# Small loads as rows on one partition, edges first in the queue, and a first tile in halves, in a GNN and FFN layer on one core

## The chip, the core and the metric

The kernel runs on one core of a Trainium2 chip. A core has TensorE (matrix products, PE in the profile, its weight loads PEld), VectorE (DVE), ScalarE (ACT), GpSimd (POOL) and SyncE (SP), each with an instruction stream of its own, worked in order; they wait for one another through semaphores. Loads and stores are issued by SP and GpSimd here and moved by 16 DMA engines. SBUF has 128 partitions; products go to PSUM. The metric is the device time of one execution in microseconds (us); less is better.

## The reference, cut to what matters

`x` is 384 x 1024 in f32. A graph attention layer and a quantised FFN are each added to it, after a layer norm without weights.

```python
x = x + gnn(_layernorm(x), [src, dst], edge_type_5, edge_type_weights, wq, bq, ... wo, bo)
x = x + ffn(_layernorm(x)[None], clip_x, clip_down, w_gate, w_up, w_down)[0]

# gnn: 16 heads of 64
q = x @ wq.T + bq                     # k and v alike
q2 = (q @ wiq.T + biq)                # k2 and v2 alike, by heads
w = softplus(edge_type_weights)       # 4 values
mask = full(-inf); mask[src, dst] = w[edge_type - 1]     # 6528 edges, the last of equal ones stays
scores = q2 @ k2.T * 0.125 + mask
out = softmax(scores) @ v2 @ wo.T + bo
# ffn: activations and weights rounded to 8 bits
scale = sigmoid(clip) * max(abs(x)) / 127                # clip: one value for x, one for the inner product
```

`edge_type_weights` has four values and the two clips one each. They are needed on all 128 partitions, as operands for each partition of later instructions.

## The kernel before

The 384 rows of `x` are three tiles of 128 rows (`NT`), the 1024 columns eight chunks of 128 (`KC`).

**The opening** (lines 83 to 358). SP issues the loads of x and of the first blocks of wq (lines 84 to 87, `load_w` at 77): x tiles 0 and 1, two blocks of wq, x tile 2, then more of wq, 512 KB each. GpSimd issues small ones (lines 100 to 105): the 40 rows of biases, the four edge weights spread to all partitions by a source that repeats (`row_bcast`, line 57), the two clips likewise, and three loads of edge indices, 51 rows of 128 values each. For each tile, `row_stats` (line 277) takes mean and variance on VectorE, a square root on ScalarE and a refinement on VectorE; `normalise` (line 284) writes the normalised row in two halves on VectorE, TensorE transposes it chunk by chunk into two PSUM tiles of four chunks, and ScalarE copies each into `xnT` (line 296). Between the two groups of a tile `normalise` calls `between`, which puts other work into the engines' streams: for tile 0 the statistics of tile 1, and for tile 1 `edges_and_stats` (line 317): the conversion of the edges, their keys, the store and loads that spread the keys, and the statistics of tile 2. `q_first` (line 300) then multiplies the tile by a block of wq: two blocks for each tile, eight products each. Each f32 product makes two records on TensorE.

Before this TensorE transposes the identity 36 times (line 311). After the third tile come the edge weights' small steps (lines 333 to 340), the transpose of the biases (line 342), the sums for the next wq pair (`left_sums`), the copy of the biases (line 346), the sums of x (`right_sums`, tile `x_right`), and the last products of the first pair (lines 349 to 358).

**Behind it** (lines 443 to 480) 15 pairs of blocks follow, seven products of half size for each (`project2`, line 189), with one step of "aside" work after each: tables for the edge weights, then the search for equal edges on VectorE (line 412) and the scatter of each 128 edges by GpSimd (line 425). The attention stage (line 541) computes scores, softmax and weighting for pairs of heads, with the last projections and the FFN's weights filled in; then come the output projection, the second norm and the FFN.

The order on TensorE, SP and GpSimd is that of the program throughout (line 74). On VectorE and ScalarE it is so from the opening to the end of line 480's loop (line 266) and again at the tail (line 726); between, a planner orders these two engines.

Of the kernel before, what the change touches and what calls it, by code (L numbers as in the profile page):

```python
# [23 lines left out]
F32 = mybir.dt.float32  # L24
# [8 lines left out]
P = 128  # L33
N = 384
NT = N // P
F = 1024
KC = F // P
# [19 lines left out]
def row_bcast(ap, n):  # L57
    return bass.AP(tensor=ap.tensor, offset=ap.offset, ap=[[0, P], [1, n]])
# [3 lines left out]
def gnn_ffn_kernel(ctx: ExitStack, tc: tile.TileContext, a: dict, out: bass.AP):  # L62
    nc = tc.nc

    const = ctx.enter_context(tc.tile_pool(name="const", bufs=1))
# [6 lines left out]
    ps_tp = ctx.enter_context(tc.tile_pool(name="ps_tp", bufs=2, space=PSUM))  # L72
# [4 lines left out]
    def load_w(name, j):  # L77
        wt = w.tile([P, F], F32, name="wt")
        nc.sync.dma_start(wt, a[name][j])
        return wt  # L80


    x = act.tile([P, NT, F], F32, name="actT")
    for t in range(NT):
        if t == NT - 1:
            wq_first = [load_w("wq", o) for o in range(FIRST)]
        nc.sync.dma_start(x[:, t, :], a["x"][t * P : (t + 1) * P, :])
    bias_rows = const.tile([5 * KC, P], F32)
    etw = const.tile([P, 4], F32)
    clip = const.tile([P, 2], F32)  # L90
    biv_b = const.tile([P, F], F32)


    ident = const.tile([P, P], F32)
# [2 lines left out]
    ph1_stack = ExitStack()  # L97
    ph1 = ph1_stack.enter_context(tc.tile_pool(name="ph1", bufs=2))
    edges_i = ph1.tile([EC, 3, P], I32, name="edges_i", bufs=1)
    nc.gpsimd.dma_start(bias_rows, a["biases"])  # L100
    nc.gpsimd.dma_start(etw, row_bcast(a["L0_gnn_edge_type_weights"], 4))
    nc.gpsimd.dma_start(clip[:, 0:1], row_bcast(a["L0_ffn_clip_x"], 1))
    nc.gpsimd.dma_start(clip[:, 1:2], row_bcast(a["L0_ffn_clip_down"], 1))
    for j, name in enumerate(("src", "dst", "edge_type_5")):
        nc.gpsimd.dma_start(edges_i[:, j, :], a[name].rearrange("(c p) -> c p", p=P))

    ahead = ph1.tile([P, GROUP * P], F32, name="ahead", bufs=1)
    nc.gpsimd.iota(ahead, pattern=[[1, GROUP * P]], base=0, channel_multiplier=-1, allow_small_or_imprecise_dtypes=True)
# [31 lines left out]

    ident_b = const.tile([P, P], BF16)
    later = ph1.tile([P, GROUP * P], F32, name="later", bufs=1)
    bias = const.tile([P, 5 * KC], F32)
    w8 = const.tile([P, 4], F32)

    def right_sums(src, pool, name, in_place=True):
# [15 lines left out]
    def left_sums(wa, wb, pool):  # L162

        half = HK * P
        s1 = pool.tile([P, half], F32, name="s1")
        s2 = pool.tile([P, half], F32, name="s2")

        def steps():
            nc.vector.tensor_add(s1, wb[:, :half], wb[:, half:])
            yield  # L170
            nc.vector.tensor_sub(s2, s1, wa[:, :half])
            yield
            nc.vector.tensor_sub(wb[:, :half], wa[:, :half], wb[:, :half])
            yield

        return (s1, s2), steps()
# [60 lines left out]
    def run(steps):  # L237
        for _ in steps:
            pass


    xnT = act.tile([P, KC, N], F32, name="actT")
# [3 lines left out]
    with ph1_stack:  # L246
# [37 lines left out]
        def normalise(t, between=None):  # L284
            xn = rows_p.tile([P, F], F32, name="row")
            for j in range(2):
                hs = slice(j * 512, (j + 1) * 512)
                nc.vector.tensor_scalar(
                    xn[:, hs], x[:, t, hs], mv1[:, t, 0:1], rstd1[:, t : t + 1], op0=ALU.subtract, op1=ALU.mult
                )  # L290
            for g in range(2):
                pt = ps_tp.tile([P, 4, P], F32, name="tp")
                for j in range(4):
                    c = 4 * g + j
                    nc.tensor.transpose(pt[:, j, :], xn[:, c * P : (c + 1) * P], ident)
                nc.scalar.copy(xnT[:, 4 * g : 4 * g + 4, t * P : (t + 1) * P], pt)
                if g == 0 and between:
                    between()

# [9 lines left out]
        pt = ps_tp.tile([P, P], F32, name="tp")  # L309
# [19 lines left out]
        q_first(0, 1)  # L329
        q_first(1, 1)  # L330
        normalise(2)

        wneg = small.tile([P, 4], F32, name="wneg")
        nc.vector.tensor_scalar(wneg, etw, -1.0, None, op0=ALU.mult)
# [3 lines left out]
        nc.scalar.activation(wexp, wnab, AF.Exp)  # L338
        wln = small.tile([P, 4], F32, name="wln")
        nc.scalar.activation(wln, wexp, AF.Ln, bias=1.0)  # L340
        pt = ps_tp.tile([P, 512], F32, name="tp")
        nc.tensor.transpose(pt[:, : 5 * KC], bias_rows, ident[: 5 * KC, : 5 * KC])
        wq_next = [load_w("wq", o) for o in (2, 3)]
        sums_next, steps = left_sums(*wq_next, ph1)
        run(steps)
        nc.vector.tensor_copy(bias, pt[:, : 5 * KC])
        x_right, steps = right_sums(xnT, ph1, "x_right", in_place=False)
        run(steps)
        q_first(0, 2)
# [2 lines left out]
        pt = ps_tp.tile([P, 3, EC], F32, name="tp")  # L352
# [102 lines left out]
        for i, (name, o) in enumerate(todo[:-1]):  # L455
# [9 lines left out]
            wq_next = [load_w(todo[i + 1][0], todo[i + 1][1] + j) for j in range(2)]  # L465
            sums_next, steps = left_sums(*wq_next, turned if todo[i + 1][0] == "wik" else ph1)
# [3 lines left out]
            if name == "wv" and o >= KC - 4:  # L470
                steps = in_turn(steps, islice(q_steps, 4))
# [69 lines left out]
    with ExitStack() as ph:  # L541
# [122 lines left out]
        for p in range(NP):  # L664
# [4 lines left out]
            if p == NP - 1:  # L669
                early = [(t, g, ps_mm.tile([P, 512], F32, name="mm")) for t, g in ((0, 0), (0, 1))]  # L670
                fill, n = (s for t, g, pm in early for s in out_group(wo, t, g, range(NP - 2), pm)), 2 * (NP - 2)
            elif p % 2:
                k2_next, fill = inner_k(p + 1)
                n = 7 * HK + 1
            else:
                fill, n = inner_v(p // 2), NT * KC
# [305 lines left out]
```

## Time and profile before

Three executions took 386.22, 386.88 and 388.01 us, median 386.88. One more, taken with the profiler, took 387.15 us; its span from the first instruction to the last is 385.4 us, so 1.75 us lie around it. The granted TensorE clock was 0.997.

| engine | busy us | share of the span | instructions |
|---|---|---|---|
| PE | 363.4 | 94% | 2100 |
| PEld | 299.4 | 78% | 2101 |
| DVE | 262.2 | 68% | 785 |
| ACT | 107.0 | 28% | 256 |
| POOL | 79.5 | 21% | 81 |

TensorE leads; in the chain that ended last it has 81% of the span, VectorE 11%, ScalarE 4%, DMA 1%. Over the first 25 us, the stage that the change edits, TensorE is busy 0.65 of the stage from 1 to 2 us (with the transposes of the identity), 0.30 of the one from 7 to 8, and full or nearly so from 11 on. A busy share over the whole span says little about this stage; it has to be read from its own lines. In a line of the timeline the columns are start, length, engine, line, operation, what it writes and reads, and, in brackets, how long the engine had been idle and what released it.

### The profile page before, as it was taken

What the parts mean: (1) busy time and instruction counts of PE and PEld (TensorE: products, weight loads), DVE (VectorE), ACT (ScalarE), POOL (GpSimd) and SP (SyncE); (2) the same over time, 40 slices, a digit from 0 to 9 for tenths busy, and PEclk for the clock granted to TensorE, in tenths of its full rate; (3) what the DMA queues carried; (4) which work ended last, traced back from release to release, by engine and by line L of the source; (5) the groups of instructions that cost most, each with busy time, mean ns of one, the idle gap of its engine ahead of it and who ended that gap; (6) DMA issues with size and microseconds to landing.
All of it is one profiled execution on the core that took longest, in us unless ns stands there. A gap on an engine that the chain in (4) does not pass through costs nothing.

```text
span 385.4 us, 5844 instructions
## 1 busy us (share of the span) xinstructions
PE 363.4 (94%) x2100; PEld 299.4 (78%) x2101; DVE 262.2 (68%) x785; ACT 107.0 (28%) x256; POOL 79.5 (21%) x81
## 2 busy tenths in 40 slices
PE   7999999999999999899899999999989999998972
PEld 7899999999999999798686767768766445457660
DVE  5878888888789977995747376546662421298775
ACT  2252100000000100325545553555243423001430
POOL 6100354454445553830000000000000000000003
PEclk9999999999999999999999999999999999999998
DMA  7996333343433355274030504050573000000004
GB/s 236 376 378 229 112 111 109 113 129 111 116 120 124 134 168 201 78 230 134 30 129 1 167 0 128 8 177 2 199 292 85 26 0 2 0 0 1 2 1 163
DMA packets 17804, 44.50 MB, mean 115 GB/s; under 512 B 3262, under 2 KB 8400, under 8 KB 17392
## 3 DMA queue, kind: packets, MB, share of 16 engines
q1 hardware_dynamic: 15104, 39.46, 30.2%
q0 software_dynamic: 2672, 4.68, 4.0%
q8 instruction: 16, 0.26, 0.3%
q14 instruction: 12, 0.10, 0.1%
HBM read 41.91 MB, written 2.21 MB: 115 GB/s over the span
## 4 chain that ended last, share of the span: by engine, by line
PE 81%; DVE 11%; ACT 4%; DMA 1%; issue 1%; POOL 0%; POOLq 0%; ACTq 0%; DVEq 0%
PE p L189 35%; PE mm L577 11%; PE mm L189 8%; PE sc L600 4%; PE sc L638 3%; PE sc L648 3%; PE mm L648 3%; PE tp L630 3%; PE mm L303 3%; DVE e L620 2%; ACT e L610 2%; ACT eTs L632 1%; PE mm L791 1%; PE x L838 1%; DVE s L606 1%
## 5 line engine op out<-in xcount | busy, mean ns | idle before, releaser
L425 POOL DMA_INDIRECT mask_d<-value,place x51 | 64.2, 1259 | 65.3 <-DVE place L422 49.9
L189 PE MATMUL p<-actT,wt 128*128 128x192 f32 x360 | 66.0, 326 | 0.5 <-DVE wt L210 0.5
L189 PEld LDWEIGHTS p<-actT,wt 128*128 128x128 f32 x360 | 59.6, 190 | 0.8 <-DVE wt L210 0.8
L577 PE MATMUL mm<-wt,actT 128*128 128x256 f32 x192 | 45.9, 386 | 0.0
L610 ACT ACTIVATE e<-s,mn 128x384 f32<-128x384 f32 x48 | 29.1, 606 | 54.3 <-DVE mn L606 54.3
L577 PEld LDWEIGHTS mm<-wt,actT 128*128 128x128 f32 x192 | 35.0, 190 | 7.9 <-issue 2.2
L606 DVE CUSTOM_DVE_ANT_0 s<-sc,mask 128x384 f32<-128x384 f32 x48 | 24.4, 552 | 14.5 <-PE sc L600 13.8
L808 POOL MEMSET hT<- 128x384 f32 x1 | 0.4, 417 | 158.6 <-PE sc L638 158.6
L189 PE MATMUL p<-x_right,s 128*128 128x192 f32 x176 | 32.2, 326 | 0.0
L189 PE MATMUL p<-x_right,wt 128*128 128x192 f32 x176 | 32.2, 326 | 0.0
L189 PEld LDWEIGHTS p<-x_right,s 128*128 128x128 f32 x176 | 29.2, 190 | 0.0
L189 PEld LDWEIGHTS p<-x_right,wt 128*128 128x128 f32 x176 | 29.2, 190 | 0.0
L632 ACT COPY eTs<-tp 128x384 f32<-128x384 f32 x48 | 20.6, 480 | 26.3 <-PE tp L630 26.2
L412 DVE SCALAR_TENSOR_TENSOR junk<-key_b,key,later 128x384 f32<-128x384 f32 (+3 forms) x51 | 27.5, 540 | 0.0
L200 DVE SCALAR_TENSOR_TENSOR actT<-p,bias,actT 128x192 f32<-128x192 f32 x45 | 18.7, 416 | 8.4 <-PE p L189 5.1
L203 ACT COPY actT<-p 128x192 f32<-128x192 f32 x15 | 4.8, 318 | 66.1 <-PE p L189 66.1
L600 PE MATMUL sc<-k,actT 64*128 64x384 f32 x96 | 22.7, 522 | 0.2 <-DVE actT L642 0.2
L630 PEld LDWEIGHTS tp<-ident,e 128*128 128x128 f32 x144 | 17.2, 140 | 4.3 <-issue 2.6
L213 ACT ACTIVATE actT<-p,bias 128x192 f32<-128x192 f32 x15 | 6.3, 421 | 50.8 <-issue 28.7
L189 PE MATMUL mm<-actT,wt 128*128 128x192 f32 x96 | 20.1, 337 | 0.3 <-ACT k L203 0.3
L501 DVE CAST wqi<-w8b 128x352 bf16<-128x352 int8 (+2 forms) x14 | 6.9, 491 | 18.8 <-PE tp L537 9.8
L630 PE MATMUL tp<-ident,e 128*128 128x128 f32 x144 | 19.6, 273 | 0.0
(210 smaller groups left out, 593.9 us busy)
## 6 DMA issues: line engine op xcount, KB each, us to landing
wt<-in_wq_dram SPq DMA_DIRECT2D x8, 512.0 KB
wt<-in_wk_dram SPq DMA_DIRECT2D x8, 512.0 KB
wt<-in_wv_dram SPq DMA_DIRECT2D x8, 512.0 KB
wt<-in_wiq_dram SPq DMA_DIRECT2D x8, 512.0 KB
wt<-in_wik_dram SPq DMA_DIRECT2D x8, 512.0 KB
wt<-in_wiv_dram SPq DMA_DIRECT2D x8, 512.0 KB
wt<-in_wo_dram SPq DMA_DIRECT2D x8, 512.0 KB
actT<-in_x_dram SPq DMA_DIRECT2D x6, 512.0 KB
```

Source lines behind the costliest of these rows:

```text
L189: nc.tensor.matmul(z, left[:, k * P : (k + 1) * P], r[:, k, :], start=(k == 0), stop=(k == HK - 1))
L200: nc.vector.scalar_tensor_tensor(dst, z, b, with_, op0=ALU.add, op1=ALU.add)
L303: nc.tensor.matmul(pm_first[o][:, ts], wq_first[o][:, k * P : (k + 1) * P], xnT[:, k, ts], start=(k == 0), stop=(k == KC - 1),)
L412: nc.vector.scalar_tensor_tensor(junk[:, :left], keys[:, (c - k0) * P : (c - k0) * P + left], key[:, c : c + 1], later[:, :left], op0=ALU. ...
L425: ins = nc.gpsimd.indirect_dma_start(out=mask_d, out_offset=bass.IndirectOffsetOnAxis(ap=place[:, c : c + 1], axis=0), in_=value[:, c : c ...
L577: nc.tensor.matmul(pm, vT[:, k, t * P : (t + 1) * P], wt[k // HK][:, k0 : k0 + 256], start=(k == 0), stop=(k == KC - 1),)
L600: nc.tensor.matmul(ps[t, h], q2[hs, t * P : (t + 1) * P], k2[hs, :], start=True, stop=True)
L606: nc.vector.tensor_tensor_reduce(s, ps[t, h], mask[:, t, :], -SCALE, 3.0e38, op0=ALU.add, op1=ALU.min, accum_out=mn[h][:, t : t + 1],)
L610: nc.scalar.activation(e[h][:, t, :], s, AF.Exp, bias=mn[h][:, t : t + 1], scale=-1.0, accum_out=sm[h][:, t : t + 1],)
L630: nc.tensor.transpose(pt[:, t * P : (t + 1) * P], e[h][:, t, m * P : (m + 1) * P], ident)
L632: nc.scalar.copy(eT[h][m], pt)
L648: nc.tensor.matmul(pm, outT[:, k, t * P : (t + 1) * P], wo[k][:, gs], start=(k == 0), stop=(k == KC - 1))
```

## The change

Loads: tile 0 of x is loaded as two halves of 512 columns. The three loads of edges go ahead of the biases in GpSimd's queue. The edge weights and the clips are loaded into one row of six values on one partition, and GpSimd fills a row of 128 ones.

Spreading: after the third tile, TensorE multiplies the ones (128 columns, one partition) by the row, which puts the six values on all 128 partitions, in the same PSUM tile as the transposed biases, beside their 40 columns. The copy into `bias` takes 46 columns, and `etw` and `clip` become slices of it. The edge weights' small steps stand behind this copy now.

Copies: for tile 0, ScalarE copies each group of four chunks in two copies of two.

```diff
-        nc.sync.dma_start(x[:, t, :], a["x"][t * P : (t + 1) * P, :])
+        for cs in (slice(0, 512), slice(512, F)) if t == 0 else (slice(0, F),):
+            nc.sync.dma_start(x[:, t, cs], a["x"][t * P : (t + 1) * P, cs])
     bias_rows = const.tile([5 * KC, P], F32)
-    etw = const.tile([P, 4], F32)
-    clip = const.tile([P, 2], F32)
+    row = const.tile([1, 6], F32)
+    ones = const.tile([1, P], F32)
...
-    nc.gpsimd.dma_start(bias_rows, a["biases"])
-    nc.gpsimd.dma_start(etw, row_bcast(a["L0_gnn_edge_type_weights"], 4))
-    nc.gpsimd.dma_start(clip[:, 0:1], row_bcast(a["L0_ffn_clip_x"], 1))
-    nc.gpsimd.dma_start(clip[:, 1:2], row_bcast(a["L0_ffn_clip_down"], 1))
     for j, name in enumerate(("src", "dst", "edge_type_5")):
         nc.gpsimd.dma_start(edges_i[:, j, :], a[name].rearrange("(c p) -> c p", p=P))
+    nc.gpsimd.dma_start(bias_rows, a["biases"])
+    for c0, n, name in ((0, 4, "L0_gnn_edge_type_weights"), (4, 1, "L0_ffn_clip_x"), (5, 1, "L0_ffn_clip_down")):
+        nc.gpsimd.dma_start(row[:, c0 : c0 + n], a[name].rearrange("(a n) -> a n", a=1))
+    nc.gpsimd.memset(ones, 1.0)
...
-    bias = const.tile([P, 5 * KC], F32)
+    NB = 5 * KC
+    bias = const.tile([P, NB + 6], F32)
+    etw, clip = bias[:, NB : NB + 4], bias[:, NB + 4 : NB + 6]
...
-                nc.scalar.copy(xnT[:, 4 * g : 4 * g + 4, t * P : (t + 1) * P], pt)
+                step = 2 if t == 0 else 4
+                for j in range(0, 4, step):
+                    c = 4 * g + j
+                    nc.scalar.copy(xnT[:, c : c + step, t * P : (t + 1) * P], pt[:, j : j + step, :])
...
         normalise(2)
+        pt = ps_tp.tile([P, 512], F32, name="tp")
+        nc.tensor.transpose(pt[:, :NB], bias_rows, ident[:NB, :NB])
+        nc.tensor.matmul(pt[:, NB : NB + 6], ones, row, start=True, stop=True)
+        wq_next = [load_w("wq", o) for o in (2, 3)]
+        sums_next, steps = left_sums(*wq_next, ph1)
+        run(steps)
+        nc.vector.tensor_copy(bias, pt[:, : NB + 6])
         wneg = small.tile([P, 4], F32, name="wneg")
         nc.vector.tensor_scalar(wneg, etw, -1.0, None, op0=ALU.mult)
...
-        pt = ps_tp.tile([P, 512], F32, name="tp")
-        nc.tensor.transpose(pt[:, : 5 * KC], bias_rows, ident[: 5 * KC, : 5 * KC])
-        wq_next = [load_w("wq", o) for o in (2, 3)]
-        sums_next, steps = left_sums(*wq_next, ph1)
-        run(steps)
-        nc.vector.tensor_copy(bias, pt[:, : 5 * KC])
```

## The prediction, made before the changed kernel was run

> **What bounds the kernel now.** I read the chain of waits first, from its start, because the change touches only the first 25 us of the span. Columns: start in us, length in us, what the chain stood in.
>
> ```profile
> 0.73 3.47 DMA actT<-in_x_dram
> 4.22 1.30 DVE st L280 x2
> 7.10 1.00 DVE row L288 x2
> 8.10 1.21 DVE st L280 x2
> 9.96 0.48 ACT actT L296
> 10.49 2.94 PE mm L303 x24
> ...
> 22.08 1.98 PE mm L303 x16
> 24.06 131.32 PE p L189 x808
> 155.53 1.11 DVE wmx L493
> ```
>
> Three things are to be seen. Up to 10.49 the chain runs through one load, VectorE and ScalarE; from 10.49 to 155.5 it is TensorE almost without a break. And it does not pass from the load of tile 0 straight into its transposes: it goes through the statistics of tile 1 (8.10) into the second copy of tile 0. The timelines of ScalarE and TensorE show why:
>
> ```profile
> 9.76 0.20 ACT L118 ACTIVATE s<-var 128x1 f32<-128x1 f32 x1 [0.78 <-DVE var L116]
> 9.87 0.57 ACT L296 COPY actT<-tp 128x512 f32<-128x512 f32 x1
> ...
> 9.04 1.16 PE L303 MATMUL mm<-actT,wt 128*128 128x128 f32 x8 [0.16 <-ACT actT L296]
> 10.49 2.94 PE L303 MATMUL mm<-actT,wt 128*128 128x128 f32 x24 [0.30 <-ACT actT L296]
> ```
>
> ScalarE works in order: the square root of tile 1 stands ahead of the copy of tile 0's chunks 4 to 7, so this copy starts only when VectorE has tile 1's variance, and TensorE stands 0.30 us for it. A gain in the opening is therefore what brings 10.49 forward, minus what is added to TensorE before 24.06.
>
> Third, the small loads on GpSimd's queue, in the table by 1 us stages (busy us and count of each engine, then granted clock, DMA share, GB/s) and the queue view of 7.0 to 7.2:
>
> ```profile
> 7.00:8.00 1.00, 0.30 (x3) 0.30 (x4) 0.96 (x3) 0.00 (x0) 0.24 (x1) 1.00 0.60 13
> ...
> q0 software_dynamic: 8, 0.00, 278.0%
> ...
> 12.34 0.35 DVE L319 CAST edges_f<-edges_i 51x384 f32<-51x384 int32 x1 [0.45 <-DMA edges_i<-in_edge_type_dram]
> 18.25 1.04 PE L295 MATMUL tp<-ident,row 128*128 128x128 f32 x8
> ```
>
> From 7 to 8 us only 13 GB/s move beside 260 and 279 around it, while eight small packets of GpSimd's queue hold the engines. The edges land only at 12.3 and hold VectorE 0.45 us. But tile 2's rows, which VectorE makes after that, end at 16.86 and TensorE takes them at 18.25: 1.4 us of slack, so neither stall is on the chain.
>
> **Part by part.**
>
> *Tile 0 in two loads.* The load is issued at 0.73 and lands at 4.20. Adding up the stages (94 KB by 2.0, 332 by 3.0, 746 by 4.0), its 524 KB have moved by 3.46, and the landing follows 0.74 later. Best case: half the bytes are through by 2.7 and land at 3.45. Worst case: time goes with rows, and a half has as many rows as the whole, so the first half lands at 4.20 and the second as much as 1.7 later (first packets at 1.75 to 3.46). The nearest row is a load of w_down at 196.2: 128 rows of 1408 bytes, through in 1.0 us. Between this and 1.7 us for rows of 4096 bytes, 2048 bytes give 1.17, so packets end at 2.92 and the half lands at 3.66. The first bn_stats then runs 3.68 to 4.3, the second needs the other half, which has the old total behind it and lands near 4.25: the pair ends some **0.52 us** earlier. Against this speaks the Trainium skill, "DMA: Bandwidth & Descriptors", Bandwidth and its rules for authors: make loads large, and two halves on one set of engines go one after the other. An estimate from its table (64 KB in 0.95 us, 1 MB in 6.15): 2.0 us for a half, 3.4 for the whole, so the second half would land 0.6 later than now, at 4.8, and the pair would end at 5.5 as before: gain nothing. The trace shows queued loads following each other at 414 GB/s without such a gap, so I take the row, and keep 0 as the other end. Price on SP's queue: one more issue of 0.43 (two take 0.86), ahead of tile 1 and all wq loads. Tile 1's bytes are through by 4.8, so it lands near 5.6 and is wanted at 7.5. wq block 1 is through at 9.2 at the earliest and is wanted at 11.47, or 10.8 after the gain. Tile 2 is through at 10.6, wanted at 12.9 now and about 12.0 then. All are bound by bytes, not by issue; cost nothing, with the least cover, some 0.5 to 1 us, at wq block 1.
>
> *Copies of tile 0 in halves.* ScalarE copies of 192 and 512 columns take 0.318 and 0.585, so 0.16 plus 0.83 ns a column: a half takes 0.37. The second group's first half is there 0.21 earlier; TensorE has 0.49 us of products (four records of 0.1225, from 2.94 for 24) before it needs the other half, which comes 0.27 later. Gain **0.20 us**, between 0 and 0.21. In the first group nothing is gained: those products end in the same wait.
>
> *Bias, weights and clips.* Three broadcast loads of 128 rows of 16 or 4 bytes become three of one row. GpSimd still issues seven loads in the same 4 us, plus one 0.1 us memset of ones ahead of the iotas, whose users come after 24 us. Edges first: they land well before 11.4, VectorE saves 0.45 us off the chain. The 13 GB/s stage goes if the etw load is its cause; if it stays on one engine, loads land as now. Bias rows and weights now come last in that queue; they are wanted at 19. On TensorE the product with ones is added between the bias transpose and the third tile's products, on the path. No row has one partition of weights; the nearest is a product record of L303, 0.1225, and an f32 product makes two records: **0.24 us**. The Trainium skill, "TensorE: Matmul & The Clock Gate", LDWEIGHTS, says that loading depends on columns and not on rows, so one partition is no discount; by its 107 ns a load the two would be 0.21. The other end is 0.1, from the edge transposes (0.32 for three).
>
> *Moved work.* wneg and wnab (0.16 each) move behind the bias copy and so behind the new product; behind them in VectorE's queue are the x_right sums. Their fourth pair is wanted by the product at 25.20 and was done near 22.9: 2.3 us cover against 0.4. On ScalarE, Exp waits for wnab; its table load (19.98 to 21.26) needs no data, and wnab comes before it ends. The next ScalarE work that TensorE needs, the copy at 25.40, follows a wait of 0.72. Cost nothing; without the cover up to 0.4 us.
>
> *Sum.* 0.52 + 0.20 - 0.24 = 0.48 us off 24.06. Nothing later runs by its own clock: weights are released by TensorE, and the edge scatter follows VectorE's work between the products. The profiled execution took 387.15 (span 385.4 and 1.75 around it), so 386.67. The median of the runs shown is 386.88, 0.27 below; the same step gives **386.4**. Half a per cent, about what a measurement of this kernel can tell from no change, is 1.9 us, so I call this the same. Its own range is 385.7 to 387.1.
>
> **The rivals.** Behind the opening, VectorE's and ScalarE's order in the attention stage is not written by hand, and a planner's order can shift when anything before it does. One place is exposed:
>
> ```profile
> 149.32 1.22 DVE L493 TENSOR_REDUCE wmx<-row 128x1 f32<-128x1024 f32 x1 [1.60 <-DMA row<-in_L_ffn_w_gate_dram]
> ...
> 158.48 1.57 PE L189 MATMUL p<-actT,wt 128*128 128x192 f32 x8 [0.52 <-DVE wt L210]
> 163.71 1.54 PE L189 MATMUL mm<-k_right,s 128*128 128x192 f32 x8 [1.05 <-DVE k_right L157]
> ```
>
> A reduction for the FFN weights stands in VectorE's queue before its row has landed; the work queued behind it makes TensorE stand 0.52 + 1.05 us.
>
> - *Faster:* the reduction moves behind the landing. 1.57 us go: 384.8. For it: nothing in the data asks for this place. Against: the opening moves all of it alike.
> - *Slower:* the reduction moves further ahead. The landing at 149.3 is tied to SP's queue, so each earlier place adds its whole distance. Behind L210 (147.2) it adds 0.4; it decides from the place ahead of L206 at 145.07, where 2.6 us more are lost: 389.0. Against it: the same.
> - *No gain:* the half tile lands as the rule has it, or the chain through tile 1 takes it back: 0 + 0.20 - 0.24, so 386.9. A late half alone, 1.7 us behind, ends the pair at 6.6 instead of 5.5: 388.0.
> - *It does not do what it says:* edges and broadcasts were never on the chain, so their part is worth nothing; this is already in my sum.
>
> **How the numbers follow.** Forecast 0.50, no gain 0.10, faster 0.22, slower 0.18. The faster case and a few good draws of the forecast make 0.24 faster; the slower one makes 0.18; 0.58 the same. The range reaches to the faster case and towards a late half, 384.4 to 388.4, and leaves out most of the slower.
>
> **What would show it.** First bn_stats at 3.7 and products of tile 0 resuming at 9.8 rather than 10.49; L189 starting near 23.6; no idle before the edge cast; no stage near 13 GB/s at 7 us; two new records of some 0.12 after the bias transpose. I am wrong if L189 starts early and the end does not move with it, or if the waits before L493, at 158 and at 164 change.

## The result, and the profile after

The changed kernel took 389.88 us in the median of ten executions (386.72 to 392.83), the kernel before beside it 386.94 (386.22 to 388.99). The ratio is 1.0061, with a 95% interval of 1.0033 to 1.009: slower by 0.6%, where 386.4 us and no measurable change were forecast. The profiled execution took 389.97 us with a span of 388.2, against 387.15 and 385.4 before: 2.8 us more. Ratios leave out slow executions, those more than 1.5% above the fastest of their kernel: one here, 392.83 us, and two of the ten of the run with tile 0 split by rows. A second timing of the same kernel, 22 executions, gave 1.0042 (below).

The chain of waits of the changed kernel, from its start (start us, length us, what the chain stood in):

```profile
0.73 0.38 SPq L88
...
2.10 7.44 DMA wt<-in_wq_dram
9.67 3.81 PE mm L311 x32
...
24.39 131.65 PE p L193 x808
```

The chain of before started with the load of x tile 0 and went through statistics and copies. This one starts with SP's issues (two halves, tile 1) and the load of wq block 0, a block whose landing no step of the prediction works out. The timelines of VectorE and TensorE show the sides of it:

```profile
3.33 0.70 DVE L284 BATCH_NORM_STATS2 st<-actT 128x6 f32<-128x512 f32 x1 [2.48 <-DMA actT<-in_x_dram]
4.91 0.69 DVE L284 BATCH_NORM_STATS2 st<-actT 128x6 f32<-128x512 f32 x1 [0.88 <-DMA actT<-in_x_dram]
...
11.99 0.34 DVE L327 CAST edges_f<-edges_i 51x384 f32<-51x384 int32 x1
...
9.67 3.81 PE L311 MATMUL mm<-actT,wt 128*128 128x128 f32 x32 [0.70 <-DMA wt<-in_wq_dram]
...
19.76 0.35 PE L342 MATMUL tp<-row,ones 1*128 1x6 f32 x2
```

The first half of tile 0 is there at 3.3 us, 0.9 earlier than the whole tile was, and VectorE then waits 0.88 us for the second: the pair ends at 5.60, before at 5.51. TensorE has tile 0's transposes behind it at 8.97 and waits 0.70 us for wq block 0. Its 32 product records then run in one piece and end at 13.48, where before they ended at 13.44. So all that the halved load and the halved copies were to bring is gone at 13.5 us, and only the product with ones (19.76, the two records) is left: the large series starts at 24.39 instead of 24.06. The cast of the edges (11.99) no longer waits.

The wait of 0.70 us is not its price. Eight of the 32 records need only the first copy of tile 0; the other 24 need the second, which still stands behind tile 1's statistics and whose first half is done at 10.41. With wq block 0 in time, TensorE would have stood for that copy, as before, and run the 24 from 10.46 to 13.40 (2.94 us each time). So the late block cost 0.08 us in this profile, and the rest of the 0.72 us forecast went on the way through VectorE: the pair came 0.61 later than forecast, and tile 1's statistics start only at 8.20, when tile 1 has just landed.

The stages of 1 us (busy us of PE, PEld, DVE, ACT and POOL with counts, granted clock, DMA share, GB/s) show what the loads did:

```profile
3.00:4.00 1.00, 1.00 (x7) 1.00 (x6) 0.67 (x1) 0.00 (x0) 1.00 (x3) 1.00 1.08 217
4.00:5.00 1.00, 1.00 (x6) 1.00 (x5) 0.12 (x2) 0.00 (x0) 1.00 (x3) 1.00 0.95 315
5.00:6.00 1.00, 1.00 (x7) 1.00 (x6) 0.93 (x3) 0.00 (x0) 1.00 (x4) 1.00 0.79 286
7.00:8.00 1.00, 1.00 (x11) 0.94 (x10) 0.96 (x3) 0.00 (x0) 0.20 (x1) 1.00 1.06 391
```

Before, these four moved 414, 370, 346 and 13 GB/s. The hole at 7 us is closed, as forecast. But the three stages behind the first half are down to 217 to 315, with the engines about as busy as before (shares 0.79 to 1.08, before 0.94 to 1.02). The trace has one landing event for each of the 16 DMA engines: of the second half, 13 engines were done by 4.08 us and the last at 4.89; of x tile 1, 15 by 6.61 and the last at 8.17, where the prediction had 5.6; of wq block 0 the last at 9.54, before at 7.70. So one engine is far behind the others for tile 1 and for the block; the events don't name the engine, so that it is the same one each time is not shown.

That accounts for 0.33 of the 2.8 us. The rest is lost at three later loads. First the changed kernel, the reduction of the gate row and the first sums of two wik pairs; then the same sums in the kernel before:

```profile
150.00 1.22 DVE L502 TENSOR_REDUCE wmx<-row 128x1 f32<-128x1024 f32 x1 [1.95 <-DMA row<-in_L_ffn_w_gate_dram]
...
169.71 0.69 DVE L173 TENSOR_TENSOR s<-wt 128x512 f32<-128x512 f32 x1 [0.28 <-DMA wt<-in_wik_dram]
...
204.16 0.69 DVE L173 TENSOR_TENSOR s<-wt 128x512 f32<-128x512 f32 x1 [3.64 <-DMA wt<-in_wik_dram]
```

```profile
168.67 0.68 DVE L169 TENSOR_TENSOR s<-wt 128x512 f32<-128x512 f32 x1
...
201.32 0.69 DVE L169 TENSOR_TENSOR s<-wt 128x512 f32<-128x512 f32 x1 [1.79 <-DMA wt<-in_wik_dram]
```

The gate row is waited for 0.35 us longer than the 1.60 of before; from there the changed kernel is 0.68 us behind. At the first wik pair, which nothing waited for before, it falls to 1.04 behind. The second wik pair is waited for 1.85 longer; from there it is 2.84, and it stays to the end. VectorE's instructions stand in the same order in both kernels, apart from the edits; only the landings differ.

### The profile page after: what moved, and what is told of

Read it like the earlier page. It is cut to its first block, busy times and chain, and to the rows that moved or that the text cites. A ratio compares the mean times of both kernels' runs of the same rounds, so it can differ in the third digit from the quotient of the medians.

```text
span 388.2 us, 5850 instructions
## 1 busy us (share of the span) xinstructions
PE 365.3 (94%) x2103; PEld 300.5 (77%) x2103; DVE 261.7 (67%) x785; ACT 107.2 (28%) x258; POOL 81.2 (21%) x82
## 4 chain that ended last, share of the span: by engine, by line
PE 77%; DVE 11%; DMA 5%; ACT 3%; issue 1%; POOL 0%; SPq 0%; POOLq 0%; ACTq 0%; DVEq 0%
PE p L193 35%; PE mm L586 10%; PE mm L193 7%; PE sc L609 4%; PE mm L657 3%; PE sc L657 3%; PE mm L311 3%; PE tp L639 3%; PE sc L647 3%; DMA wt<-in_wq_dram 2%; DMA wt<-in_wik_dram 2%; DVE e L629 2%; ACT eTs L641 1%; ACT e L619 1%; PE mm L800 1%
## 5 line engine op out<-in xcount | busy, mean ns | idle before, releaser
L434 POOL DMA_INDIRECT mask_d<-value,place x51 | 65.9, 1292 | 63.9 <-DVE place L431 45.2
```

The lines of the kernel that those rows point to most:

```text
L434: ins = nc.gpsimd.indirect_dma_start(out=mask_d, out_offset=bass.IndirectOffsetOnAxis(ap=place[:, c : c + 1], axis=0), in_=value[:, c : c ...
```

## The experiments

All ratios below are to the kernel before on the same chip, unless a run is said to be a single profiled execution. The order of every engine's instructions was the same as in the kernel each one starts from, apart from its edit.

**How far the ratios can be trusted.** The kernel before, timed as if it were another:

> The kernel before, unchanged, timed as if it were another. It shows how far the ratios of this study can be trusted and how much its own profile varies. If the method is sound: 1.000, within 0.002. In its profile, theory 1 (landings vary from execution to execution) expects a wait of VectorE for the gate row between 1.3 and 2.5 us and a landing of wq block 0 between 7.7 and 9.3; the rival (the kernel before always lands them in time) expects 1.6 and 7.7.

387.75 us, 1.0015 (1.0004 to 1.0026). The true value is 1, so an interval can be off by some 0.15%: below, 1.002 is not told from no change. The gate row was waited for 1.6 us in this profile too and the second wik pair 1.46, but wq block 0 landed at 8.68 instead of 7.70 and the transposes ahead of tile 0 took longer (see the warm-up below). The granted clock is no rival for the whole: its mean over the executions is 0.994 for the changed kernel, for the halves alone and for the kernel before beside them.

**The change once more, and one part at a time.** The same kernel:

> The changed kernel once more, for a second profile. Start theory (the two half loads start the stream of loads badly, a hiccup at 3.3 to 4.3 us and one DMA engine left behind): again the second half lands after 4.5, wq block 0 lands near 9.6 and TensorE stands for it at 9; L193 starts near 24.2 or later. Chance theory (a DMA engine falls behind anywhere, the change only makes more of the program wait on loads): the opening looks different this time, and the 7 us landing of wik at 197 is elsewhere or gone. Time 388 to 391 either way.

389.13 us, 1.0042 (1.0021 to 1.0062). Its profile has the wait for wq block 0 again (0.73 us, products from 9.41), the halves at 3.35 and 4.57, the series from 24.13. But its second wik pair is waited for only 1.58 us, and its span is 386.5, 1.7 shorter than that of the first profile. So the opening repeats and the late second wik pair does not. With the block in time this profile would have ended its 32 records at 13.14 instead of 13.22, so the late block is worth 0.08 us again.

The kernel before with tile 0 in halves and nothing else:

```diff
-        nc.sync.dma_start(x[:, t, :], a["x"][t * P : (t + 1) * P, :])
+        for cs in (slice(0, 512), slice(512, F)) if t == 0 else (slice(0, F),):
+            nc.sync.dma_start(x[:, t, cs], a["x"][t * P : (t + 1) * P, cs])
```

> Kernel before with tile 0's load alone in halves. Start theory: slower by 1 to 3 us, with the second half after 4.5. Small-loads theory (edges first and one-partition rows do the harm): faster by 0.3 to 0.5 us, as the sum of the prediction has it for this part.

390.46 us, 1.0081 (1.0051 to 1.0112): more than the whole change. The timelines of this kernel, VectorE, ScalarE and TensorE, and its stages:

```profile
3.51 1.46 DVE L281 BATCH_NORM_STATS2 st<-actT 128x6 f32<-128x512 f32 x2 [2.65 <-DMA actT<-in_x_dram]
9.48 1.28 DVE L281 BATCH_NORM_STATS2 st<-actT 128x6 f32<-128x512 f32 x2 [1.50 <-DMA actT<-in_x_dram]
...
11.34 0.57 ACT L297 COPY actT<-tp 128x512 f32<-128x512 f32 x1
...
11.04 1.13 PE L304 MATMUL mm<-actT,wt 128*128 128x128 f32 x8 [1.98 <-DMA wt<-in_wq_dram]
...
6.00:7.00 1.00, 1.00 (x7) 1.00 (x6) 0.89 (x4) 0.00 (x0) 1.00 (x4) 1.00 0.68 181
7.00:8.00 1.00, 1.00 (x11) 1.00 (x10) 0.97 (x2) 0.00 (x0) 0.23 (x1) 1.00 0.82 59
```

Here the forecast of the pair came true: it ends at 4.97, 0.54 us before the pair of the kernel before. It is worth nothing, since the next two loads on the queue are both late. x tile 1, forecast near 5.6, lands at 9.45; so the second copy of tile 0 ends only at 11.91, and TensorE could run its last 24 records no earlier than from 11.95 to 14.89. wq block 0 lands at 10.91, TensorE shows a wait of 1.98 us for it, and its 32 records end at 14.90: either late load alone would have given the same end. The slow stream of the halves (270 and 280 GB/s from 3 to 5 us) and the hole of the broadcast loads (181 and 59) now stand in a row in front of both. The series starts at 25.50, 1.44 us late; the other 1.8 us of this profile's loss come at the first wik pair (below).

The change without the halves:

```diff
-        for cs in (slice(0, 512), slice(512, F)) if t == 0 else (slice(0, F),):
-            nc.sync.dma_start(x[:, t, cs], a["x"][t * P : (t + 1) * P, cs])
+        nc.sync.dma_start(x[:, t, :], a["x"][t * P : (t + 1) * P, :])
```

> Changed kernel with tile 0's load whole. Start theory: same as the kernel before, or up to 0.3 us better; x tile 0 lands at 4.2. Small-loads theory: slower by 1 to 3 us.

388.06 us, 1.0015 (0.9995 to 1.0035): not told from the kernel before. The stream is at 397, 381 and 344 GB/s again, TensorE doesn't wait for wq block 0, its products run from 8.75 and 10.21, and the series starts at 24.05.

The row on one partition and the product with ones alone, edges last, tile 0 whole:

```diff
-    nc.gpsimd.dma_start(etw, row_bcast(a["L0_gnn_edge_type_weights"], 4))
...
+        nc.gpsimd.dma_start(row[:, c0 : c0 + n], a[name].rearrange("(a n) -> a n", a=1))
...
+        nc.tensor.matmul(pt[:, NB : NB + 6], ones, row, start=True, stop=True)
```

> Kernel before with only the edge weights and clips as a row on one partition and the product with ones; the edges stay last. Start theory: plus 0.25 us (the product), not measurable. Small-loads theory: slower by 1 us or more, with one DMA engine late for wq blocks 0 and 1.

388.73 us, 1.0029 (1.001 to 1.0047), at the edge of what can be told. From 6 to 8 us the loads move 403 and 395 GB/s, so it is the broadcast loads that made the hole; the series starts at 24.32, 0.26 after that of before, the price of the product. The profile of this run was its longest execution, 392.26 us, and has a late second wik pair although tile 0 came whole; TensorE's granted clock then drops (the column behind the five counts):

```profile
204.32 0.69 DVE L171 TENSOR_TENSOR s<-wt 128x512 f32<-128x512 f32 x1 [3.32 <-DMA wt<-in_wik_dram]
...
210.00:220.00 10.00, 9.41 (x53) 7.69 (x53) 3.67 (x14) 6.32 (x15) 0.00 (x0) 0.85 0.13 36
```

The record of the clock has it at 0.5 from 209.5 to 212.9 us. So a late second wik pair does not need the halves.

The edges first, alone:

```diff
+    for j, name in enumerate(("src", "dst", "edge_type_5")):
+        nc.gpsimd.dma_start(edges_i[:, j, :], a[name].rearrange("(c p) -> c p", p=P))
     nc.gpsimd.dma_start(bias_rows, a["biases"])
...
-    for j, name in enumerate(("src", "dst", "edge_type_5")):
-        nc.gpsimd.dma_start(edges_i[:, j, :], a[name].rearrange("(c p) -> c p", p=P))
```

> The kernel before with the three edge loads ahead of the other loads in GpSimd's queue; nothing else. The prediction on record costs this at nothing: VectorE stops waiting for the edges before their cast, the end stays, ratio 1.000 within 0.0015. Rival (edges landing late in some executions hold up the kernel before, as at 13.1 us in the run with the late start): ratio 0.997 to 0.999. Other rival (the broadcast of the edge weights, now later in the queue, stalls the stream where wq block 1 and tile 2 are loaded): ratio 1.001 to 1.003.

387.08 us, 0.9999 (0.9988 to 1.0011): nothing, as forecast. The hole is not gone but moved with the broadcasts: 66 and 226 GB/s from 8 to 10 us.

The kernel before with 512 bytes more in its constants:

```diff
+    spare = const.tile([P, 128], F32)
+    nc.vector.memset(spare[:, 0:1], 0.0)
```

> The kernel before with 512 bytes more per partition in its pool of constants, so that the tiles allocated after it lie 512 bytes higher, as the new constants of the change leave them; nothing else. If the placement is what makes later landings late: ratio 1.002 to 1.004 as in the run with rows only. If it is not: 1.000, within 0.0015, and that run's 0.3% belongs to its loads and its product or to nothing that can be told.

387.16 us, 1.0001 (0.9983 to 1.0018). Placement, as far as these 512 bytes test it, is out. In this profile wq block 0 landed at 9.18 and TensorE waited 0.51 us for it although tile 0 came whole: the kernel before has little to spare there in some executions.

**What it is in the halves.** Two halves of 64 partitions instead of 512 columns, in the changed kernel:

```diff
+        for r0, r1 in ((0, 64), (64, P)) if t == 0 else ((0, P),):
+            nc.sync.dma_start(x[r0:r1, t, :], a["x"][t * P + r0 : t * P + r1, :])
```

> The changed kernel with tile 0 in two loads of 64 partitions of 4 KB each, instead of two loads of 128 partitions of 2 KB. Theory 1 (a second load behind the first on the queue leaves DMA engines behind, whatever the size of its pieces): the stream from 3 to 6 us runs at 200 to 320 GB/s again, x tile 1 lands near 8, TensorE waits 0.7 us or more for wq block 0, ratio 1.004 to 1.006. Rival (the 2 KB pieces do it): the stream runs at 345 to 420 GB/s, tile 1 lands near 5.5, no wait for wq block 0, ratio near 1.0015 as with the tile whole.

391.92 us, 1.0083 (1.005 to 1.0117), so the rival falls: pieces of 4 KB do it too. The profile is of the second longest of its ten executions, 394.22 us; only its landings are read here. VectorE's first statistics, which need both halves here:

```profile
5.33 1.29 DVE L284 BATCH_NORM_STATS2 st<-actT 128x6 f32<-128x512 f32 x2 [4.48 <-DMA actT<-in_x_dram]
```

The second half lands 1.1 us after the whole tile did. Part of that is a price of its own: SP's issues are 0.62 us apart instead of 0.44, and no bytes move before 2 us. The stream is at 250 and 243 GB/s from 3 to 5 us; TensorE did not wait for wq block 0, since the chain was late already. Theory 1 was right about the slow stream and wrong about the place.

The second half on ScalarE's queue:

```diff
+            q = nc.scalar if cs.start else nc.sync
+            q.dma_start(x[:, t, cs], a["x"][t * P : (t + 1) * P, cs])
```

> The changed kernel with the second half of tile 0 issued on ScalarE's DMA queue, so SP issues tile 1 right behind the first half. Theory 1 (two short loads one behind the other on one queue leave engines behind): second half lands near 3.9, tile 1 near 5.6, wq block 0 near 7.8 and not waited for, first products near 9.9; end 0.5 us earlier than with the tile whole, ratio near 1.000 (0.998 to 1.001). Rival (the 2 KB pieces make the engines fall behind, on whichever queue): tile 1 near 8, TensorE waits for wq block 0, ratio 1.004 to 1.006.

388.27 us, 1.0021 (1.0004 to 1.0038), not told from no change. The stream runs at 445 and 401 GB/s from 3 to 5 us, and nothing waits for wq block 0:

```profile
4.08 1.29 DVE L285 BATCH_NORM_STATS2 st<-actT 128x6 f32<-128x512 f32 x2 [3.23 <-DMA actT<-in_x_dram]
```

Both halves are there at 4.08 or soon after, about when the whole tile comes (4.22 before, 4.15 and 4.05 in two runs above). Two halves with the same pieces, side by side, do no harm that can be told and bring nothing. So for the slow stream neither the size of the pieces nor the number of half loads is enough: it takes the two half loads one behind the other on SP's queue. Why two of 256 KB do what a row of 512 KB loads on the same queue does not, no run shows. This run differs in one more way from the changed kernel: SP's queue has no load more than before.

wq block 0 ahead of x tile 1, halves kept:

```diff
-        if t == NT - 1:
-            wq_first = [load_w("wq", o) for o in range(FIRST)]
+        if t > 0:
+            wq_first.append(load_w("wq", t - 1))
```

> The changed kernel, tile 0 still in two halves, with wq block 0 issued ahead of x tile 1 and wq block 1 ahead of x tile 2. Theory 1 (what the halves cost is TensorE's wait for wq block 0 behind a slow stream): wq block 0 lands before 9.0 us, the 0.7 us wait goes, x tile 1 may land as late as 8.5 without being on the path, the large series starts at 23.9 or earlier, ratio to the kernel before 1.000 to 1.002 as with tile 0 whole. Rival A (tile 1, now third in the queue, lands after 9.3 and takes the place of wq block 0): start later than 24.4, ratio 1.004 or more. Rival B (the halves cost elsewhere, later in the kernel): start 23.9 and the ratio still 1.004 to 1.006.

391.16 us, 1.0111 (1.0092 to 1.0131), rival A, and more than it asked. The chain of waits:

```profile
2.10 6.84 DMA actT<-in_x_dram
8.96 1.30 DVE st L285 x2
11.23 2.94 PE mm L312 x24
```

The series starts at 25.08. Tile 1 lands at 8.9 and takes the place of the block: its statistics stand ahead of the copy of tile 0's second group. In both orders the load that comes fourth is late.

**A later landing that comes with the halves.** Behind the opening, one wait parts the kernels with two halves on SP's queue from all others: that for the first wik pair. SP's issues of a row of w_up and of the pair, before and in the changed kernel, and VectorE's first sum of the pair in the halves alone (second profile):

```profile
161.95 0.33 SPq L514 DMA_DIRECT2D row<-in_L_ffn_w_up_dram  x1
162.38 1.19 SPq L79 DMA_DIRECT2D wt<-in_wik_dram  x2
...
162.63 0.33 SPq L523 DMA_DIRECT2D row<-in_L_ffn_w_up_dram  x1
163.44 0.80 SPq L79 DMA_DIRECT2D wt<-in_wik_dram  x2
...
169.56 0.69 DVE L170 TENSOR_TENSOR s<-wt 128x512 f32<-128x512 f32 x1 [1.44 <-DMA wt<-in_wik_dram]
```

In the eight profiles with such halves the first block is issued 0.48 to 0.52 us behind the row, in the twelve others 0.10 or 0.11. The pair has landed 7.0 to 8.4 us after the row's issue, against 6.35 to 7.0, and VectorE waits 0.28 to 1.70 us for it (mean 1.05), against 0 to 0.30 (mean 0.08). Measured against the kernel before, the eight fall back by 0.35 to 1.78 us between the gate row and this sum (mean 1.1), the others by at most 0.37 (mean 0.15). It is the largest piece of the loss that repeats. The issue order is the same; what differs is that SP's queue has one load more, and with it every later load tells of its landing on the next semaphore of the row that they use in turn (the pair on 117 and 118 instead of 116 and 117). The second half on ScalarE's queue leaves the 0.10 as it was. Whether the one load more does this or the slow stream no run parts: a load more on SP's queue with tile 0 whole would.

**What a late start costs.** 13 idle transposes on TensorE ahead of the bias transpose, in the kernel before and then in the kernel with edges first:

```diff
+        pt = ps_tp.tile([P, P], F32, name="tp")
+        for _ in range(13):
+            nc.tensor.transpose(pt, ident, ident)
         pt = ps_tp.tile([P, 512], F32, name="tp")
         nc.tensor.transpose(pt[:, : 5 * KC], bias_rows, ident[: 5 * KC, : 5 * KC])
```

> The kernel before with 13 idle transposes put on TensorE right before the transpose of the bias rows; no load is touched. Four transposes take 0.45 us in the kernel before, so 13 take about 1.45 us; 0.24 us of them fill an idle gap, and the large product series should start near 25.1 instead of 23.9. Theory 1 (a late start costs what it is late, once): end later by 1.2 us, ratio 1.003. Rival (a late start also makes the wait for the wik pair at 160 to 172 us longer, so halves cost twice): end later by about 2.9 us, ratio 1.0075, with VectorE waiting more than the 1.8 us of before for wik. Third (the late start is absorbed at a later landing): ratio within 0.001 of 1.

389.64 us, 1.0064 (1.0045 to 1.0084). In its profile the edges landed only at 13.1 us as well, so its start (26.48) is not a clean dose. The second run is:

> The kernel with edges first and, as in the run with the late start, 13 idle transposes on TensorE ahead of the transpose of the bias rows (1.64 us there, of which 0.24 us fill a gap). Compared with the kernel that has edges first alone. Theory 1 (a late start costs what it is late, once; the late start of the earlier run cost more because its edges landed late too): 1.4 us more than edges first, 0.0036 in the ratio. Rival (a late start makes later landings cost more): 2.5 us more, 0.0065 in the ratio.

389.85 us, 1.0072 (1.0055 to 1.0089), 0.0073 above edges first alone. VectorE's first sum of the second wik pair:

```profile
203.90 0.69 DVE L169 TENSOR_TENSOR s<-wt 128x512 f32<-128x512 f32 x1 [2.88 <-DMA wt<-in_wik_dram]
```

The series starts at 25.46, 1.57 us after that of edges first, and the median is 2.8 us up: near the rival's numbers. Once more the second wik pair is waited for longer (2.88 against 1.50). Is it the lateness? The same lateness by ScalarE, which repeats copies of the same data to the same place:

```diff
                 nc.scalar.copy(xnT[:, 4 * g : 4 * g + 4, t * P : (t + 1) * P], pt)
+                if (t, g) == (2, 1):
+                    for n in (4, 4, 2):
+                        nc.scalar.copy(xnT[:, 4 : 4 + n, t * P : (t + 1) * P], pt[:, :n])
```

> Edges first, and three more copies on ScalarE (of the same data to the same place) ahead of TensorE's last products of the opening: two of 0.59 us and one of about 0.37, so the main stage starts about 1.5 us late, as in the two runs with 13 transposes, but TensorE's program is not longer by one instruction. Theory 1 (lateness alone makes later landings cost more): ratio to the kernel before 1.006 to 1.0075, as in those runs. Rival (their excess came from 26 more records in TensorE's program, which move its instruction fetches against the weight loads): 1.5 us, ratio 1.0035 to 1.0045, and the second wik pair is waited for 1.5 to 1.9 us as in the kernel before.

388.21 us, 1.002 (1.0008 to 1.0032). The second wik pair in this kernel:

```profile
201.97 0.69 DVE L169 TENSOR_TENSOR s<-wt 128x512 f32<-128x512 f32 x1 [1.27 <-DMA wt<-in_wik_dram]
```

The series starts at 24.94, only 1.05 us late, as part of the copies ran beside other work, and the median is 0.8 us above that of edges first by the ratios. At this dose, two thirds of the other, lateness is paid once. So the excess of the transposes is hardly lateness; either it is their place in TensorE's program, or something that came with it. In the late executions one of the 16 engines delivers the last wik block alone, 1.6 to 1.9 us after the other 15 (landing events of the changed kernel, of rows alone and of the run with edges first and transposes). A 16 KB packet of queue 8, instructions, runs in the same stretch, but in the kernel before as well, so what holds that engine is not shown. Over all twenty profiles the second pair is waited for 2.3 to 3.6 us in six, two of them with halves and four without, and 1.3 to 1.9 us in the others.

**The warm-up.** 23 instead of 36 transposes of the identity, with edges first (`WARM = 23`):

> Edges first with 23 instead of 36 transposes in the warm-up, whose end at 6.9 us is not on the path; the program of TensorE becomes 26 records shorter, and no useful work moves. If the place of instruction fetches against the second wik pair matters: a change of 1 us or more in either direction, ratio outside 0.998 to 1.002, and the wait for the second wik pair other than 1.5 to 1.9 us. If it does not: 1.000 within 0.0015.

386.64 us, 0.9983 (0.9971 to 0.9994): a small gain, just between the two theories. Two more single profiled executions, of the changed kernel and of the halves alone:

> One more look at the changed kernel. Theory 1 (the halves delay wq block 0 each time): TensorE waits 0.5 us or more for wq block 0, and the main stage starts at 24.1 or later. Rival (this was one execution's bad luck): no wait, start near 23.7.

> One more look at the kernel before with tile 0 in halves and nothing else. Theory 1 (halves and the broadcast's stall add up): TensorE waits 1.5 us or more for wq block 0, start after 25. Rival (chance): wait under 0.7, start near 24.

The halves alone again waited for wq block 0 (1.29 us), less than theory 1 asked, with the series from 24.45; by tile 1, 0.46 us late for VectorE, it would have been the same within 0.01. The changed kernel had no such wait, and yet started at 24.31. Its chain of waits, then TensorE's transposes of the opening by stages of 1 us (busy with count, granted clock, DMA share, GB/s):

```profile
1.34 7.11 PE tp L319 x36
8.46 0.87 PE tp L299 x8
9.46 3.95 PE mm L311 x32
...
4.00:5.00 1.00, 1.00 (x6) 1.00 0.90 241
...
8.00:9.00 1.00, 1.00 (x12) 1.00 1.02 365
```

The counts take in each record that reaches into a stage. By their starts in the trace, the transposes follow each other every 213 or 214 ns up to some moment and every 109 ns from then on, a step of 1.95. In the kernel before the step comes at 4.38 us and the 36 take 5.59 us; here it comes at 7.53, they take 7.11, and they end after the rows of tile 0 are ready. The table prints a granted clock of 1.00 throughout, but the trace's record of the clock begins only at 4.34 us before and at 7.46 here, just ahead of the step, and within 0.11 us of it in all seventeen profiles with 36 transposes; ahead of it nothing is recorded. The Trainium skill, "TensorE: Matmul & The Clock Gate", Part 1, has a clock that doubles after a busy window of about 3.4 us which runs free of the kernel's start, and so opens at another moment in each execution. The step agrees; the page's spread of half a microsecond does not, as it comes 3.0 to 6.2 us after the first transpose here. The kernel before, in its second profile, took 6.83 us for them and had them on its chain too, at no loss: its series began at 24.02.

The changed kernel with 23, to part the two causes:

> The changed kernel with 23 warm-up transposes instead of 36, so that the warm-up ends by 6.4 us and can't hold TensorE. Theory 1 (the loss is the late wq block 0 behind the halves): TensorE still waits for wq block 0, main stage at 24.1 or later, ratio to the kernel before 1.003 to 1.006, at most 0.002 better than the changed kernel. Rival (a late warm-up, or the place of TensorE's program, makes the loss): ratio 0.998 to 1.001.

388.59 us, 1.0024 (1.0007 to 1.0041), between the two theories; its executions had a lower granted clock than the kernel before beside them (mean 0.992 against 0.995), so part of even this may not be the halves. Nothing waits for wq block 0 in this profile (products from 8.71); the pair of statistics ends at 5.39 behind the second half. Last, the parts that cost nothing, put together: edges first, copies in halves, 23 transposes, tile 0 whole, broadcasts kept.

```diff
-                nc.scalar.copy(xnT[:, 4 * g : 4 * g + 4, t * P : (t + 1) * P], pt)
+                step = 2 if t == 0 else 4
+                for j in range(0, 4, step):
+                    c = 4 * g + j
+                    nc.scalar.copy(xnT[:, c : c + step, t * P : (t + 1) * P], pt[:, j : j + step, :])
```

> The kernel before with the edges first, the copies of tile 0 on ScalarE in halves and 23 warm-up transposes; tile 0 whole and the broadcast loads kept. Theory 1 (these parts help or cost nothing when the load stays whole): main stage near 23.7, 0.2 us before the run with edges first and 23 transposes, ratio 0.997 to 0.9985. Rival (the gain of 23 transposes was an accident of that run): 1.000 within 0.0015.

386.48 us, 0.9976 (0.9962 to 0.9991). It is below both kernels, by 0.24% of the one before, little more than the 0.15% by which the control was off. Beside the changed kernel with 23 transposes, timed together with it, it is 0.5% ahead, and the intervals do not meet: what differs is the halved load and the row with its product, and the product is 0.3 us of those 2. Its series starts at 23.70, 0.36 us before that of the kernel before.

## Why the prediction was wrong, step by step

**Tile 0 in two loads: -0.52 us. This step failed.** In four profiles of the changed kernel's opening (36 transposes in three, 23 in one) the pair of statistics ends at 5.60, 5.27, 5.69 and 5.39, with the tile whole at 5.24 to 5.51 in eleven: no gain. That is the end of the range that the prediction worked out from the Trainium skill, "DMA: Bandwidth & Descriptors", Bandwidth, and set aside with the words that "the trace shows queued loads following each other at 414 GB/s without such a gap". That row was read from whole tiles. Behind a half the stream fell to 217, 315 and 286 GB/s, and the half forecast "near 4.25" came at 4.57 to 5.00. The first half was forecast at 3.66 and came at 3.3 to 3.4. In the kernel with the halves alone the 0.52 did come (0.54), so the estimate of the half was not the whole of the error.

**"All are bound by bytes, not by issue; cost nothing, with the least cover at wq block 1." This failed too**, and it is what takes the gain away where there is one. Tile 1, forecast near 5.6 and wanted at 7.5, landed at 8.17 in the changed kernel and at 9.45 with the halves alone; wq block 0, which the list leaves out, landed at 9.54 and 10.91 instead of 7.70. TensorE's waits of 0.70 and 1.98 us for the block show the second of these, but the copy behind tile 1's statistics would have held it to within 0.08 and 0.01 us of the same end. For the changed kernel the forecast of -0.72 (0.52 and 0.20) became +0.04 at 13.5 us: 0.61 lost with the pair, about 0.08 up to tile 1's statistics, 0.08 at the block.

**Copies in halves: -0.20.** Right: the start of the series is 23.70 in the last run and 23.89 with the same kernel without them.

**Product with ones: +0.24.** A little small: in the chains its two records take 0.31, and the third tile's products start 0.56 us after the bias transpose instead of 0.26.

**Edges first and the hole at 7 us.** Right: the wait before the cast is gone, the end doesn't move (0.9999), and the hole goes with the broadcast loads (403 and 395 GB/s without them). That this would help wq block 0 was not seen: the halves alone, with the hole, waited 1.98 and 1.29 us for it, the changed kernel 0.73 or less.

**"Nothing later runs by its own clock." Failed.** The start is at 24.13 to 24.39 in three profiles instead of 23.6, a miss of 0.55 to 0.8 us of the 3.3 between 386.67 forecast and 389.97 measured. The other 2.5 come from the landings of the gate row (0.35), of the first wik pair (0.35) and of the second (1.8 by the offset at 204), which the sum took as tied to TensorE. In two further profiles of the changed kernel the second pair is not late, and their spans are 386.5 and 385.7: that part changes from execution to execution, and it comes without halves too. The first pair is late in all of them (0.28, 0.67 and 1.46 us).

**What is shown and what is open.** That the two halves on SP's queue carry most of the loss rests on four ratios: 1.0081 with the halves alone, 1.0042 to 1.0061 with the whole change, 1.0015 without the halves, 1.0021 with the second half on another queue. Singly, the last three lie close to what can be told, and rows alone gave 1.0029. Two things repeat in every profile with such halves: a slow stream in the opening, and a first wik pair that lands some 1.1 us later. The opening costs 0.07 to 0.33 us of the start in the changed kernel; how the halves reach the wik pair, by the stream or by the one load more on SP's queue, is open. What makes the second pair late now and then is open as well: not the order of instructions, nor placement as far as tested, nor the halves. 13 transposes more cost 0.3% beyond their time, 13 fewer bring 0.17% with no earlier start in the profile, and the changed kernel goes from 1.0042 or 1.0061 to 1.0024 with 23; this points to TensorE's warm-up or program against the loads, but no run parts those two.

**The rivals.** The order of the reduction did not change, so neither the faster nor the slower rival happened. "No gain" had the right end of the half tile, and, for a half 1.7 us late, a time of 388.0 through the statistics; the late loads were tile 1 and a weight block. None of the rivals had those.

## What to carry to other kernels

When a load is cut in two, look at what stands behind it in the same queue: list every load there with its landing and the moment it is wanted, the next two first. A wait that the profile shows is not yet a price: ask what the engine would have waited for next had this load been in time. A half that comes early is worth something only if the second half and the next load come no later; two halves on different queues cost nothing here that could be told, and brought nothing. And where a profile shows several loads landing within a microsecond of being wanted, a sum over the chain is good to no better than that, and one profile says little about the median.

## What the runs showed of the hardware that was not expected

- Two half loads of 256 KB one behind the other on one queue slowed the stream: from 3 to 4 us it moved 180 to 270 GB/s in all eight profiles with such halves, and 377 to 445 in the others, the one with two queues among them. By 6 us, adding up the stages, 1.06 to 1.23 MB had moved with them, and 1.30 to 1.55 MB in the others. In five of the eight, one to five of the 16 engines delivered tile 1 late, up to 3.6 us behind the rest; in the other three none lagged by more than about half a us. Engines up to 1.8 us behind the others occur with the tile whole too, for wq block 0.
- In the same eight the first wik pair, 160 us later, was waited for 1.05 us in the mean, in the other twelve 0.08.
- The three broadcast loads of 16 or 4 bytes to each of 128 partitions, 3 KB in all, pulled a stage of 1 us down to between 12 and 180 GB/s in every kernel that kept them, wherever they stood in the queue; the kernels without them had no stage under 300 from 6 to 10 us. Which of the three does it was not tested.
- 36 transposes of 128 x 128 took 5.6 to 7.1 us in the same place: one every 213 ns up to a step between 4.4 and 7.5 us, one every 109 ns from then on. The table's granted clock of 1.00 ahead of the step stands for no record.
